# Four-layer image kernel on one Trainium2 core: group norms that hand over to the other image between their steps

## The chip, the cores and the metric

The kernel runs on one core of a Trainium2 chip. The metric is device time in microseconds of one execution, lower being better. The engines named below are PE (matrix products; PEld is its weight load), DVE (vector work out of SBUF and PSUM), ACT (ScalarE: functions and scaled copies), POOL (GpSimd) and SP (SyncE, which here only issues DMA transfers).

## The reference

Four images of 32 x 32 pixels and 384 channels pass through four layers, each of the form x = x + layer(gn(x)), where gn is a group norm over 32 groups of 12 channels and all pixels of an image:

```python
def _gn(v, G=32, eps=1e-5):
    B_, H_, W_, C_ = v.shape
    g = v.reshape(B_, H_, W_, G, C_ // G)
    m = jnp.mean(g, axis=(1, 2, 4), keepdims=True)
    s = jnp.var(g, axis=(1, 2, 4), keepdims=True)
    return ((g - m) / jnp.sqrt(s + eps)).reshape(v.shape)
...
x = x + _L0_conv_ref(_gn(x), ...)
x = x + _L1_conv_ref(_gn(x), ...)
x = x + _L2_conv_ref(_gn(x))
x = x + _L3_conv_ref(_gn(x), ...)
```

Layer 0 is deformable attention: a grouped 3 x 3 convolution of the queries gives offsets, keys and values are sampled at them, and six heads of 64 channels attend over 1024 x 1024 positions with a sampled bias. Layer 1 is attention with twelve heads of 32 channels, whose weights are multiplied by a group similarity (twelve heads are worked in six pairs). Layer 2 divides a squared box sum by a box sum of squares. Layer 3 gives each pixel a softmax over its 3 x 3 neighbourhood, applied to values and added back. All is float32, and no image depends on another.

## The kernel before

The images are independent, so the program runs two of them side by side. The *front* computes layer 0 of one image (`Front.layer0`), the *trunk* computes layers 1 to 3 of the image before it (`Trunk.image`). Layer 0 of image 0 comes first, with part of image 1's front. Then trunk 0 runs beside front 1, trunk 1 beside front 2, trunk 2 beside front 3, and trunk 3 alone.

Both sides are Python generators. A `yield n` ends a piece of the program and says that it is worth n steps. `Net.layer3` weaves the two: after each piece of the trunk it emits pieces of the front until the front is a tenth of an image ahead, counting 1109 steps for a trunk and 714 for a front:

```python
for w in self.trunk.image(b, out):
    self.done += w / TRUNK_STEPS
    while self.ahead < self.done + LEAD:
        self.ahead += next(self.fronts, 1.0)
```

The order in which instructions are emitted is not yet the order on an engine. A scheduler takes emission as priority: on each engine it places, at each point, the earliest emitted instruction that by its own reckoning is ready and has room for its output, so later pieces can fill in. On the chip each engine then runs its queue strictly in the placed order. Buffers are tiles in pools, and an allocation waits until the former holder of the space is done with.

A group norm is `Lane.norm_steps` (L342 to L394), itself a generator with a bare `yield` between steps. Where the statistics are not given it first takes them on DVE, three channel blocks (`stats`, L328 and L329). Then two small steps on DVE (L357, L358), seven tiny products on PE with the group matrix `gmat`, which sum the statistics over groups (L362), three places to hand over, the mean and variance on DVE (L372 to L375), a square root on ACT (L378), four places to hand over, the reciprocal (L380), and for each of three channel blocks a place to hand over and the normalisation on DVE (L386). `Lane.norm` runs all of it without a handover.

The norms of the program and what stands around them:

- Trunk, layer 1 (`image`): norm in place in the tile `whole`, as one piece, 15 steps. Then `inputs1`: three gate products (`dense_t`, L407) with nine filter taps each, query and key products (L1396) and so on. Then six pairs (`pair`): for each of eight key blocks j two half turns of 7 steps, with the products of queries and keys (L1699) into a two-bank PSUM tile `big`, of which there are two; exponentials (L1707); products of similarities (L1729); the weighting (L1736); products with the values (L1671). Beside it, for the next pair, `sums_step` makes products into `big` (L1561), their maximum on DVE (L1570) and the exponential's sum on ACT (L1574), which frees `big`.
- Trunk, layer 2: `out1` adds the layer 1 output (L1803, L1815) and takes the statistics; norm into `xp` as one piece, 15 steps; sums of neighbours on DVE (L1838) and PE (L1845), box products (L1870), and the result added to x (L1912, L1913) with the statistics for layer 3.
- Trunk, layer 3: norm into `xh` as one piece; products with `Wa` (L1935) and their copy (L1942); only then 15 steps; softmax, value products (L421), the sum over neighbours (L2058). At its end `start` loads the next image's x and `gmat`.
- Front, `normed`, images 2 and 3: loads of the image (L583), 24 transposes (L604) with copies (L609), a store of x on ACT's queue (L613), the norm, all as one piece of 25 steps; then transposes of the normalised image (L628) and stores (L642). Then three projections (L407), three convolution pieces (L667, 36 products and 15 steps each), and later the heads: four window pieces of 6 steps each (POOL gathers, ACT and DVE interpolate, L956 to L971, products L968), a maximum, then exponentials and value products (L1001 to L1003). Two half heads of 38 steps take as long by the weights as one pair. After every second head the sums are divided (`over_sums`). `outputs0` ends a front: output products (L407), residual loads (L491), addition (L496) and stores (L497).

The front's image 1 has its norm inside `Early`, beside image 0, and hands over there already (`alone`).

Of the kernel before, what the change touches and what calls it, by code (L numbers as in the profile page):

```python
# [27 lines left out]
NB, HW, C = 4, 32, 384  # L28
# [401 lines left out]
class Front(Lane):  # L430
# [146 lines left out]
    def normed(self, b):  # L577

        nc = self.nc
        xin = self.wt([P, NJ, C], "a12", 2)  # L580
        src = self.a["x"][b].rearrange("(j p) c -> p j c", p=P)
        for j in range(0, NJ, 2):
            nc.sync.dma_start(xin[:, j : j + 2, :], src[:, j : j + 2, :])  # L583
        if b == 0:
            early = self.early_lane
            early.gm, early.wq = self.weights("gmat"), self.weights("w_q")
            early.taps = [self.conv_weights(0)]
            self.net.more_consts()
            self.windows()
            next(self.early)  # L590
            early.taps += [early.conv_weights(1), early.conv_weights(2)]
        if b == 0:
            x = self.net.first = self.net.trunk.whole()[1]
        else:
            x = self.wt([P, KC, N], "a12", 2)

        alone = b == 1
        if alone:
            for _ in range(4):
                yield  # L600
        for j in range(NJ):
            ps = self.bank()
            for k in range(KC):
                nc.tensor.transpose(  # L604
                    ps[:, k * P : (k + 1) * P], xin[:, j, k * P : (k + 1) * P], self.ident
                )
            if alone:
                yield
            nc.scalar.copy(  # L609
                x[:, :, j * P : (j + 1) * P], ps[:, 0:C].rearrange("p (k n) -> p k n", k=KC)  # L610
            )
        if b > 0:
            nc.scalar.dma_start(self.x0[b % 2].rearrange("(k p) n -> p k n", p=P), x)  # L613
        xh = self.wt([P, KC, N], "a12", 2)
        gmat = self.gm if b == 1 else self.early_lane.gm if b == 0 else None
        for _ in self.norm_steps(x, xh, None, gmat):
            if alone:
                yield
        if b == 0:
            self.borders()  # L620
        yield 25


        pv = self.pairs[b % 2].rearrange("(g s) (y c) -> y s g c", g=G, y=2)
        for j in range(NJ):
            ps = self.bank()
            for k in range(KC):
                nc.tensor.transpose(  # L628
                    ps[:, k * P : (k + 1) * P], xh[:, k, j * P : (j + 1) * P], self.ident
                )  # L630
            if alone:
                yield
            if b == 1:
                xn = self.wt([P, C], "xn", 2)
            else:
                if j % 4 == 0:
                    four = self.wt([P, G, 2, 2 * GC], "gat", 3)
                    four = four.rearrange("p g l c -> p (g l c)")
                xn = four[:, j % 4 * C : (j % 4 + 1) * C]
            nc.scalar.copy(xn, ps[:, 0:C])  # L640
            for y, first in ((0, HW + 1), (1, 1)):
                nc.sync.dma_start(  # L642
                    pv[y, first + j * P : first + (j + 1) * P],
                    xn.rearrange("p (g c) -> p g c", g=G),
                )
        return xh
# [667 lines left out]
class Trunk(Lane):  # L1314
# [16 lines left out]

    def image(self, b, out):
        x, gmat = self.begun
        self.norm(x, x, None, gmat)
        self.xh = x
        yield 15
        with self.scope("l1y"):


            self.q4, self.k4 = self.wt([P, N], "q4"), self.wt([P, N], "k4")  # L1340
            self.xg = self.wt([P, N], "xg")
            yield from self.layer1(b)
            yield from self.layers23(b, out)
# [476 lines left out]
    def layer2(self):  # L1820
        nc, v = self.nc, self.nc.vector
        with self.scope("l2"):
            xp = self.wt([P, KC, HW, HW + 4], "xp")
            for lo in (0, HW + 2):
                nc.gpsimd.memset(xp[:, :, :, lo : lo + 2], 0.0)
            self.norm(self.x, xp[:, :, :, 2 : 2 + HW], self.mv[0])
            yield 15
            band = self.weights("band")
            num, den = [], []

# [34 lines left out]
            def box20(src, ko):  # L1865
                ps = self.big()
                near = [k for k in range(KC) if abs(k - ko) <= 1]
                for q in range(2):
                    for k in near:
                        nc.tensor.matmul(  # L1870
                            ps[:, q * 512 : (q + 1) * 512],
                            band[:, k, ko * P : (ko + 1) * P],
                            src[k][:, q * 512 : (q + 1) * 512],
                            start=k == near[0],
                            stop=k == near[-1],
                        )
                return ps
# [32 lines left out]
            for ko in range(KC):  # L1910
                psn, dn, x = box20(num, ko), dns[ko], self.x[:, ko, :]
# [6 lines left out]
    def layer3(self, b, out):  # L1918
        nc, v = self.nc, self.nc.vector
        skew = self.skew[b % 2]  # L1920
        with self.scope("l3"):
            xh = self.wt([P, KC, N], "xh")
# [2 lines left out]
            apad = self.wt([81, PW, PW], "apad")  # L1925
            nc.gpsimd.memset(apad, 0.0)
            w = self.weights("Wv")
            self.norm(self.x, xh, self.mv[1])
            attn = self.wt([P, NJ, 81], "attn")
            mt = self.wt([P, NJ, C], "mt")  # L1930
            lt = mt.rearrange("p j c -> p (j c)")[0:81, 0:N]
            for h in range(2):
# [9 lines left out]
                nc.scalar.activation(  # L1942
                    lt[:, h * 512 : (h + 1) * 512], ps, AF.Identity, bias=self.ba[:, 0:1]
                )
            yield 15
            av = attn.rearrange("p j (a q) -> p (j a) q", q=9)
            red = self.wt([P, NJ * 9], "red")
            for h in range(2):
# [204 lines left out]
```

## Time and profile before

| | us |
|---|---|
| runs shown | 4333.46, 4356.05, 4359.73 (median 4356.05) |
| profiled execution, device time | 4376.54 |
| its span | 4374.6 |
| PE busy | 3934.7 |
| DVE busy | 3109.3 |
| ACT busy | 2306.0 |
| mean granted PE clock | 0.954 |

Layer 0 of image 0 takes the first 514 us, up to the first normalisation of trunk 0 (L386 into `whole`). The next such normalisations are at 1580.0, 2655.4 and 3684.6 us, so a trunk with a front beside it takes 1066, 1075 and 1029 us and the last trunk alone some 690.

In the views below a line of the timeline reads: start, duration, engine, line, operation, output<-inputs, shape, count, and in brackets the idle time of that engine before it and what ended it. A line of the waits reads: who waited <- for whom, total us, times, longest. A float32 product shows as two instructions in the profile. Idle time matters only on the engine that holds the others up at that place.

### The profile page before, as it was taken

Reading aid. Unit: us, or ns where it says so; the run is one execution under the profiler, and the core shown is the slowest. Engines: PE = TensorE matmul, PEld = TensorE weight load, DVE = VectorE, ACT = ScalarE, POOL = GpSimd, SP = SyncE. Lnnn points to the kernel's source line nnn. Section 1 sums busy time; section 2 is a strip of 40 time slices with the busy share of each in tenths; the row PEclk is TensorE's granted clock in tenths of the full one; section 3 lists DMA queues with packets and bytes.
Section 4 is the critical chain, followed back from the end, with each engine's and each line's share of the span. In section 5 each row is a group of like instructions: output and inputs, shape, how many; then the busy total and the mean of one; then the engine's idle time right before and its main releaser. Section 6 shows DMA issues by size and latency. Waiting matters only on the chain.

```text
span 4374.6 us, 45298 instructions
## 1 busy us (share of the span) xinstructions
PE 3934.7 (90%) x14832; PEld 1683.2 (38%) x14832; DVE 3109.3 (71%) x5905; ACT 2306.0 (53%) x3638; POOL 959.2 (22%) x979
## 2 busy tenths in 40 slices
PE   8788989898999898889899989889989999999998
PEld 4333434333334443433333443333333334344444
DVE  4699676878787456687878836578887874566654
ACT  3276445656664334466766423366676641566633
POOL 1655152212121105221212101431121301000000
PEclk9999989999999998999999999899999999999998
DMA  7643253113221354321222154432221214311111
GB/s 159 220 124 119 75 177 95 55 48 93 55 85 40 123 137 146 110 64 42 78 57 80 40 158 142 130 100 61 57 79 47 74 34 135 103 38 30 33 33 43
DMA packets 295397, 385.08 MB, mean 88 GB/s; under 512 B 167858, under 2 KB 228798, under 8 KB 294650
## 3 DMA queue, kind: packets, MB, share of 16 engines
q1 hardware_dynamic: 246336, 217.44, 17.7%
q0 software_dynamic: 39936, 145.53, 11.3%
q10 hardware_dynamic: 8890, 19.23, 1.3%
q8 instruction: 118, 1.93, 0.2%
q14 instruction: 117, 0.96, 0.1%
HBM read 295.63 MB, written 86.75 MB: 87 GB/s over the span
## 4 chain that ended last, share of the span: by engine, by line
PE 50%; DVE 25%; issue 9%; ACT 9%; DMA 3%; POOL 2%; another core or an unknown queue 1%; SPq 0%; ACTq 0%; DVEq 0%; POOLq 0%
PE bank L1729 10%; PE big L1699 6%; PE big L407 5%; DVE nmax L1570 4%; PE bank L1003 4%; DVE e L1736 3%; PE big L1561 3%; ACT big L1574 3%; PE bank L421 3%; PE bank L1724 2%; PE bank L1396 2%; PE bank L1671 2%; DVE lg L962 2%; DVE z L957 2%; PE big L1870 2%
## 5 line engine op out<-in xcount | busy, mean ns | idle before, releaser
L1729 PE MATMUL bank<-whole,sg 128*128 128x512 f32 (+3 forms) x2304 | 851.7, 500 | 3.4 <-POOL sg L1682 1.8
L1736 DVE SCALAR_TENSOR_TENSOR e<-bank,gam,e 128x512 f32<-128x512 f32 x768 | 560.0, 746 | 308.7 <-PE bank L1729 184.2
L1574 ACT ACTIVATE big<-big,nmax 128x1024 f32<-128x1024 f32 x384 | 417.5, 1087 | 286.1 <-DVE nmax L1570 249.8
L1729 PEld LDWEIGHTS bank<-whole,sg 128*128 128x128 f32 x2304 | 399.6, 196 | 354.8 <-issue 272.8
L1699 PE MATMUL big<-qa,ka 64*128 64x512 f32 x1536 | 450.5, 666 | 87.8 <-ACT big L1574 84.7
L1570 DVE TENSOR_REDUCE nmax<-big 128x1 f32<-128x1024 f32 x384 | 451.8, 1216 | 68.3 <-PE big L1561 64.7
L1707 ACT ACTIVATE e<-big 128x1024 f32<-128x1024 f32 x384 | 381.8, 1020 | 176.0 <-PE big L1699 164.6
L944 POOL DMA_INDIRECT win<-strips,widx x288 | 314.3, 1091 | 697.1 <-DVE z L957 378.8
L1682 POOL TENSOR_SCALAR sg<-whole,gam 128x512 f32<-128x512 f32 x192 | 149.7, 780 | 1350.1 <-PE bank L1729 1070.4
L1561 PE MATMUL big<-k,q 32*128 32x512 f32 x1536 | 268.1, 661 | 37.5 <-issue 15.9
L1003 PE MATMUL bank<-lg,va 128*128 128x512 f32 x576 | 269.7, 610 | 13.7 <-ACT lg L1002 13.7
L751 POOL DMA_INDIRECT gat<-pairs,sidx x192 | 210.3, 1095 | 325.3 <-DVE ix_one L550 237.6
L1699 PEld LDWEIGHTS big<-qa,ka 64*128 64x128 f32 x1536 | 147.9, 197 | 344.0 <-ACT big L1574 179.1
L962 DVE SCALAR_TENSOR_TENSOR lg<-z,bias_f,lg 128x512 f32<-128x512 f32 x288 | 216.4, 768 | 49.5 <-ACT lg L961 46.8
L956 ACT ACTIVATE z<-win,bias_f 128x528 f32<-128x528 f32 x288 | 205.5, 736 | 57.4 <-DVE lg L962 26.2
L1001 DVE TENSOR_TENSOR lg<-lg,tb 128x512 f32<-128x512 f32 x288 | 181.9, 689 | 73.7 <-ACT tb L994 73.7
L957 DVE SCALAR_TENSOR_TENSOR z<-win,bias_f,z 128x528 f32<-128x528 f32 x288 | 215.0, 763 | 19.8 <-ACT z L956 11.8
L1671 PE MATMUL bank<-e,vs 128*32 128x512 f32 x1536 | 210.9, 618 | 16.8 <-DVE vs L1665 16.7
L1741 ACT COPY gn<-bank 128x128 f32<-128x128 f32 (+2 forms) x288 | 106.4, 370 | 210.6 <-DVE e L1736 209.7
L961 ACT ACTIVATE lg<-z,bias_f 128x512 f32<-128x512 f32 x288 | 199.7, 716 | 16.6 <-DVE z L957 12.1
L971 DVE TENSOR_TENSOR lg<-bank,lg 128x512 f32<-128x512 f32 x288 | 191.1, 681 | 12.1 <-PE bank L968 11.7
L968 PE MATMUL bank<-qs,kz 64*128 64x512 f32 x288 | 168.6, 669 | 13.2 <-DVE e L1736 8.3
(326 smaller groups left out, 6328.7 us busy)
## 6 DMA issues: line engine op xcount, KB each, us to landing
q<-qd SPq DMA_DIRECT2D x48, 256.0 KB
xg<-xgd SPq DMA_DIRECT2D x48, 256.0 KB
pairs<-gat SPq DMA_DIRECT2D x48, 192.0 KB
w<-in_gmat SPq DMA_DIRECT2D x15, 576.0 KB
w<-in_Wqkv SPq DMA_DIRECT2D x12, 576.0 KB
a<-in_x SPq DMA_DIRECT2D x16, 384.0 KB
q<-qpad SPq DMA_DIRECT2D x12, 512.0 KB
qs<-q SPq DMA_DIRECT2D x24, 256.0 KB
```

What stands on the lines that cost most here:

```text
L944: nc.gpsimd.indirect_dma_start(out=win, out_offset=None, in_=self.strips[:, :], in_offset=bass.IndirectOffsetOnAxis(ap=self.widx[:, q, c : ...
L957: v.scalar_tensor_tensor(z, wv[:, 1 : HH + 1, 0 : HW + 1], sc(0, 1), z, ALU.mult, ALU.add)
L962: v.scalar_tensor_tensor(lg, z[:, :, 1 : HW + 1], sc(0, 0), lg, ALU.mult, ALU.add)
L1003: nc.tensor.matmul(po, self.values_of(h, j), lf, start=j == 0, stop=j == NJ - 1)
L1561: nc.tensor.matmul(ps[r][:, h * 512 : (h + 1) * 512], self.q4[rows, i * P : (i + 1) * P], self.k4[rows, 0:512], start=True, stop=True,)
L1570: top = v.tensor_reduce(nmax[:, r, i : i + 1], ps[r], AX.X, ALU.max, negate=True)
L1574: nc.scalar.activation(ps[r], ps[r], AF.Exp, bias=nmax[:, r, i : i + 1], accum_out=den[:, r, i : i + 1],)
L1671: nc.tensor.matmul(av[r0 : r0 + HD1, :], vs[:, r, :], es[h][:, r, :], start=j == 0, stop=j == NJ - 1,)
L1699: nc.tensor.matmul(ps[:, r, :], ka[rows, j * P : (j + 1) * P], qa[rows, cols], start=True, stop=True,)
L1707: nc.scalar.activation(e, ps, AF.Exp)
L1729: last = nc.tensor.matmul(ps[:, (mid - i0) * P :], sg[:, r, m, :], sim[:, h, r, m, (mid - i0) * P :], start=m == 0, stop=m == 1,)
L1736: v.scalar_tensor_tensor(e[:, r, :], ps, self.gam[:, 1:2], e[:, r, :], ALU.add, ALU.mult, accum_out=tot[:, r, h : h + 1],)
```

## The change

The trunk's three norms, and the front's norm for images 2 and 3, now hand over at each place that `norm_steps` offers: 13 places where the norm takes its own statistics (trunk layer 1, front), 10 where they are given (layers 2 and 3). The step weights are 1 per place in layer 1 (13 in all, 15 before), 1.5 in layers 2 and 3 (15 in all), and 2 in the front (26 in all, 25 before). In layer 3 the piece with the `Wa` products keeps 2 steps. The counts 1109 and 714 by which the two sides are paced stay.

```diff
@@ -616,9 +616,12 @@
         for _ in self.norm_steps(x, xh, None, gmat):
             if alone:
                 yield
+            elif b > 1:
+                yield 2
         if b == 0:
             self.borders()
-        yield 25
+        if b < 2:
+            yield 25
@@ -1331,9 +1334,9 @@
     def image(self, b, out):
         x, gmat = self.begun
-        self.norm(x, x, None, gmat)
+        for _ in self.norm_steps(x, x, None, gmat):
+            yield 1
         self.xh = x
-        yield 15
         with self.scope("l1y"):
@@ -1823,8 +1826,8 @@
-            self.norm(self.x, xp[:, :, :, 2 : 2 + HW], self.mv[0])
-            yield 15
+            for _ in self.norm_steps(self.x, xp[:, :, :, 2 : 2 + HW], self.mv[0]):
+                yield 1.5
             band = self.weights("band")
@@ -1925,7 +1928,8 @@
             w = self.weights("Wv")
-            self.norm(self.x, xh, self.mv[1])
+            for _ in self.norm_steps(self.x, xh, self.mv[1]):
+                yield 1.5
             attn = self.wt([P, NJ, 81], "attn")
@@ -1942,7 +1946,7 @@
-            yield 15
+            yield 2
             av = attn.rearrange("p j (a q) -> p (j a) q", q=9)
```

Lines behind the first edit stand three further down in the changed kernel (L1835 becomes L1838), from layer 3's product with `Wa` on four (L1935 becomes L1939).

## The prediction

> **What bounds the kernel now.** I read the page first, then PE's waits, then the stretches around the norms, then PE's order in time there.
>
> ```profile
> span 4374.6 us, 45298 instructions
> ...
> PE 3934.7 (90%) x14832; PEld 1683.2 (38%) x14832; DVE 3109.3 (71%) x5905; ACT 2306.0 (53%) x3638; POOL 959.2 (22%) x979
> ```
>
> PE is busy for 90% of the span, so an edit that only reorders work can save no more than PE's idle time, 4374.6 - 3934.7 = 440 us, and what a lower clock costs. PE's waits, longest in total:
>
> ```profile
> PE big L1699 <- ACT big L1574: 84.7, 46, 5.1
> ...
> PE bank L1935 <- DVE xh L386: 13.9, 4, 3.5
> PE bank L362 <- DVE gn_mv L358: 13.7, 4, 5.6
> ...
> PE bank L362 <- issue: 8.8, 2, 4.4
> ...
> PE big L407 <- DVE whole L386: 4.3, 2, 2.1
> ```
>
> The norms (L362, and readers of L386) are small entries. The largest entry belongs to the six attention pairs of layer 1, where a product waits for PSUM that ScalarE frees. PE around the layer 3 norm of image 0, with the norm of image 2 (the layer 0 side, "front" below) behind it:
>
> ```profile
> 1477.26 1.70 PE L362 MATMUL bank<-gn_mv,w 128*128 128x2 f32 x14 [0.37 <-DMA w<-in_gmat]
> 1482.44 7.68 PE L1935 MATMUL bank<-xh,Wa 128*81 128x512 f32 x12 [3.49 <-DVE xh L386]
> 1489.96 2.98 PE L604 MATMUL bank<-ident,a 128*128 128x128 f32 x24
> 1497.35 3.09 PE L362 MATMUL bank<-gn_mv,w 128*128 128x2 f32 x14 [4.41 <-issue]
> ```
>
> Two holes, 3.49 and 4.41 us: each norm is one piece, and PE has nothing else in its queue. SyncE's queue in the same place:
>
> ```profile
> 1478.24 0.34 SPq L497 DMA_DIRECT2D x<-res  x1
> 1478.99 0.37 SPq L257 DMA_DIRECT2D w<-in_w_q  x1
> 1482.46 1.92 SPq L583 DMA_DIRECT2D a<-in_x  x4
> ```
>
> and what the DMA engines did then (columns: stretch, its length, busy time of PE, PEld, DVE, ACT, POOL, granted clock, DMA share, GB/s):
>
> ```profile
> 1485.60:1488.40 2.80, 2.80 (x6) 0.97 (x5) 0.00 (x0) 0.68 (x1) 0.00 (x0) 0.72 1.00 375
> 1488.40:1490.00 1.60, 1.60 (x6) 0.48 (x5) 0.00 (x0) 0.00 (x0) 0.00 (x0) 1.00 0.01 2
> ```
>
> The load of the next front image (L583) starts 4.2 us after the last store of the front before it (L497) and moves data until 1488.4. That matters below.
>
> **The change, part by part.** No instruction is added or removed: all engines keep the same number of each, activation table loads included. In the built programs PE's order differs in 208 stretches, DVE's in 364, ACT's in 232, SP's in 78, POOL's in 26. Durations below are from the profiled execution, 4376.5 us on the device; the median of the three runs is 4356.05, so a sum made on it is multiplied by 4356.05/4376.54 = 0.9953 at the end.
>
> Layer 1 norm, images 1 and 2. Before, PE has the third convolution piece (L667, 7.96 us) right behind the norm's sums and never idles. By the step weights that piece now comes due only after the first gate product (L407), and in the built order L407 stands right behind the sums. It must wait for the norm. Image 3, which has no front, shows the price: 2.12 us (the L407 entry above, two cases, 4.3 us). The clock there:
>
> ```profile
> 1580.00:1590.00 10.00, 10.00 (x72) 3.76 (x65) 2.25 (x3) 1.27 (x2) 4.97 (x6) 1.00 0.46 135
> ...
> 3676.00:3686.00 10.00, 7.88 (x34) 5.41 (x33) 6.58 (x18) 0.30 (x1) 0.00 (x0) 0.97 0.38 123
> 3686.00:3696.00 10.00, 10.00 (x21) 4.29 (x21) 0.87 (x2) 2.17 (x2) 7.25 (x8) 0.86 0.18 68
> ```
>
> Covered (image 1, first line) it is 1.00; uncovered (image 3) 0.97 and 0.86, so 0.3 + 1.4 = 1.7 us of PE work are lost. 2 x (2.1 + 1.7) = +7.6. The lower end is 0.
>
> The Trainium skill ("TensorE: Matmul & The Clock Gate", section "HAM oscillation — how this bites in real kernels") says that gaps above about 3.4 us are what halves the clock. By it a hole of 2.1 us costs no clock and this term would be +4.2. The row speaks against it.
>
> Layer 2 norms, images 0 to 2. The norm's sums now stand in the middle of eight front products (L1003) instead of behind them. Before, the readers (L1845) wait 2.25 us, three times 6.8, at clocks of 0.83, 0.83 and 0.66 over 10 us (1.7 + 1.7 + 3.4 = 6.8 us). With four products, 8 passes x 0.44 = 3.5 us, moved behind the sums that hole can close. But the sums may now wait for their statistics: from the last L1803 (ended 1384.45) to the second gn step (ended 1389.29) were 4.8 us, and only 3.5 us of products stand there, 1.3 too few. Ends: -13.6 and 3 x 1.3 = +3.9. Since the front's DVE work stays in between, I take -0.5 each, -1.5.
>
> Layer 3 norm and front norm, image 0. The new order puts the 24 transposes (L604) ahead of L1935 to fill the hole. They need the loads, which stay behind the same store: first quarter there at about 1485.6 (384 KB at 343 GB/s from 1484.3), last at 1488.4. From 1479.0 to the end of the last quarter's transposes (1488.4 + 2.98/4 = 1489.2) PE has 10.2 us with 2.98 of work: 7.2 idle, against 3.49 + 4.41 = 7.9. The front's sums come after L1935 and the value products (L421, 9.34 us) and no longer wait. -0.7. One long hole in place of two also spares one of two stretches of 6.8 us at half clock (0.72, 0.94 and 0.66 over 1476 to 1506): -3.4, at worst 0.
>
> The same, image 1. Before: 1.04 + 3.48 + 4.40 = 8.9 idle. After, the norm's sums stand behind only two L407 (4 passes, 1.8 us) after the last box product, while their statistics took 4.5 us there in image 0 (1471.74 to 1476.27): 2.7 idle. Fourteen L407 follow, then the transposes: from the last L407 (ended 2552.3) to the end of the loads (2563.5) and the last quarter (0.75) are 12.0 us, 9.0 of them idle. 11.7 - 8.9 = +2.8, and -3.4 of clock as above: -0.6.
>
> Image 2, layer 3 (no front left). Six L407 (5.3 us) now stand behind the sums and cover the 3.49; the clock there was 0.66 over 10 us: -3.5 - 3.4 = -6.9.
>
> SP: in image 0 the load of the group matrix (gmat) moves ahead of the residual loads (L491) and waits there for the last band product; the residuals took 5.1 us to arrive, and six L407 (5.3 us) cover that. 0, and 5.1 if not. Queued behind are the stores of L497 and the loads of L583.
>
> Attention pairs, images 0 to 2. Layer 1's norm now counts 13 steps, not 15, and each front image 715, not 714. In the pairs the front therefore lags by 2 trunk steps in image 0, 3.6 in image 1, 5.1 in image 2, out of 7 per half turn: some 30, 50 and 70% of the front's pieces move by one half turn. No trace shows that order. But the old pairs themselves lie at two lags, as the front's division of its sums takes 3.1 steps after the second pair: PE idle is 14.1 and 13.1 in pairs 1 and 2, 14.3 and 10.7 in pairs 3 and 4. Lag moves the mean by 1.1 us per pair; 15 pairs, 16 us either way. I take 0.
>
> Sum: 7.6 - 1.5 - 4.1 - 0.6 - 6.9 = -5.5. 4376.5 - 5.5 = 4371.0, times 0.9953: 4351. Ends: best 0 - 13.6 - 4.1 - 0.6 - 6.9 - 16 = -41, worst 7.6 + 3.9 - 0.7 + 2.8 - 3.5 + 5.1 + 16 = +31: 4315 to 4387.
>
> **Rivals.** *All holes close* (faster): if the loads arrive in time and the pieces fit, the idle time goes: 15.8 in the layer 3 pairs of norms, 3.5 in image 2, 6.8 in layer 2, together 26; and the clock behind it, 6.8 + 5.1 + 3.4 + 6.8 = 22. -48: 4308. For it: pieces do land in the holes. Against: L583 behind L497, and the lost cover in layer 1.
>
> *The pairs get worse* (slower): front work on DVE delays the maxima (L1570), ScalarE frees PSUM later (L1574), and L1699 waits. Price: the old pairs differ by 14.33 - 10.66 = 3.7 us; 15 times 55 us: 4376.5 - 5.5 + 55, times 0.9953: 4405. It decides from (43.6 + 5.5)/15 = 3.3 us per pair, or 27 waits of the present mean (84.7/46 = 1.84). For it: the largest wait is of this kind. Against: lags already present differ by only 1.1.
>
> *The scheduler filled these holes already, and nothing changes*: 4356. The order differs, and the holes are there; little speaks for it.
>
> **The numbers.** 1%, 43.6 us, is about what a measurement of this kernel can tell from no change. Forecast 0.50, no effect 0.06, all holes close 0.20, pairs worse 0.24. So within 1%: 0.56, faster 0.20, slower 0.24. The likeliest case is 4351 with 4315 to 4387; to leave out no more than 2 in 10, the range goes past both rivals: 4300 to 4410.
>
> **What would show it.** Layer 1 norms of images 1 and 2: L407 waits 2.1 us for L386. Image 0, layer 3: L604 waits some 6.6 us for L583, and neither L1939 (the old L1935) nor the front's L362 waits. Pairs: 117 to 124 us each, L1699 waiting 70 to 100 us in all. Wrong if pairs move by more than 3 us each, or if L604 finds its data at once.

## The result, and the profile after

The changed kernel takes 4398.46 us (median of 6 runs, 4390.75 to 4404.67), the kernel before, measured beside it, 4344.99 (6 runs, 4331.74 to 4359.73). The ratio is 1.0123, with an interval of 1.0104 to 1.0142: slower by 53.5 us. The time lies inside the predicted range, but only because that was drawn wide enough to take in the rivals: the likeliest case (4351, within 1%) did not happen. The rival "the pairs get worse" had 4405.

The page of the changed kernel (span, then busy time and instructions of each engine):

```profile
span 4392.7 us, 45243 instructions
...
PE 3933.9 (90%) x14832; PEld 1689.1 (38%) x14832; DVE 3111.1 (71%) x5905; ACT 2314.6 (53%) x3638; POOL 966.6 (22%) x979
```

Each engine's count is that of before and its busy time within 1%; what changed is mostly waiting. PE's waits (total us, times, longest), line numbers are three higher from L622 on and four from L1929 on:

```profile
PE big L1702 <- ACT big L1577: 88.8, 61, 4.4
PE big L1564 <- ACT big L1577: 34.0, 13, 7.0
PE bank L993 <- POOL diag L991: 28.7, 29, 5.8
PE bank L604 <- DMA a<-in_x: 25.9, 3, 11.3
PE bank L1006 <- ACT lg L1005: 25.8, 23, 2.4
...
PE bank L362 <- DVE gn_mv L358: 15.1, 5, 5.7
...
PE big L407 <- DVE whole L386: 8.7, 4, 2.2
```

The same entries before:

```profile
PE bank L990 <- POOL diag L988: 22.8, 29, 1.3
...
PE big L1561 <- issue: 15.9, 9, 4.1
...
PE bank L1003 <- ACT lg L1002: 13.7, 11, 2.4
...
PE big L1561 <- ACT big L1574: 8.9, 5, 4.1
...
PE bank L604 <- DMA a<-in_x: 6.9, 1, 6.9
```

Over the whole kernel the top entry hardly grew (84.7 before). The front's value products L1006 and its diagonal L993 wait longer, and so do the front's transposes L604. The sums' product L1564 seems to (34.0 against 8.9), but before the change another 15.9 us of its waits are put down to "issue", and the kernel with the handovers alone (first experiment below), which loses no time, has 27.5; of L604 it has 20.8. The waits of Wa's product fell from 13.9 to 3.5 us (image 3, which has no front), that of L362 for nothing but its place (8.8) is gone, and L407's doubled.

The places the prediction named, in PE's order. Image 0, layer 3 norm and front norm:

```profile
1480.40 1.62 PE L362 MATMUL bank<-gn_mv,w 128*128 128x2 f32 x14
1493.34 4.30 PE L604 MATMUL bank<-ident,a 128*128 128x128 f32 x24 [11.32 <-DMA a<-in_x]
1497.48 5.31 PE L1939 MATMUL bank<-xh,Wa 128*81 128x512 f32 x12
...
1512.56 1.62 PE L362 MATMUL bank<-gn_mv,w 128*128 128x2 f32 x14
```

The order is as forecast: one hole instead of two, neither L1939 nor the front's L362 waits. The hole is 11.32 us instead of some 6.6. SyncE's queue says why:

```profile
1480.59 0.38 SPq L257 DMA_DIRECT2D w<-in_gmat  x1
1482.04 0.38 SPq L257 DMA_DIRECT2D w<-in_w_q  x1
1483.83 0.34 SPq L497 DMA_DIRECT2D x<-res  x1
1489.07 1.91 SPq L583 DMA_DIRECT2D a<-in_x  x4
```

The store now starts 3.4 us after the norm's sums (1.0 before), and the load 5.2 us behind the store (4.2 before). Layer 1 norm of image 1:

```profile
1579.90 1.72 PE L362 MATMUL bank<-gn_mv,w 128*128 128x2 f32 x14
1583.86 7.08 PE L407 MATMUL big<-whole,w 128*128 128x512 f32 x12 [2.23 <-DVE whole L386]
1590.88 7.96 PE L670 MATMUL big<-qpad,w 64*64 64x512 f32 x72
```

The convolution piece L670 fell behind the product whose wait it used to cover, as forecast. The 10 us around that hole and around the one in image 2 (columns as in the stretches below):

```profile
1580.00:1590.00 10.00, 7.77 (x25) 4.21 (x26) 2.92 (x7) 1.56 (x3) 0.00 (x0) 0.83 0.37 118
...
2661.70:2671.70 10.00, 7.76 (x24) 4.25 (x24) 2.92 (x7) 1.56 (x3) 0.00 (x0) 0.66 0.38 118
```

And the five attention pairs behind the first in image 0 (stretch, its length, busy time of PE, PEld, DVE, ACT, POOL with instruction counts, granted clock, DMA share, GB/s), first before:

```profile
781.17:903.35 122.18, 108.04 (x438) 43.84 (x437) 100.39 (x196) 81.09 (x131) 26.23 (x26) 0.99 0.23 66
903.35:1026.69 123.34, 110.20 (x442) 44.27 (x441) 96.39 (x190) 77.18 (x124) 20.56 (x22) 0.96 0.20 55
1026.69:1148.88 122.19, 107.86 (x435) 43.41 (x435) 105.25 (x203) 85.86 (x138) 30.76 (x31) 0.97 0.28 80
1148.88:1267.76 118.88, 108.22 (x439) 43.11 (x441) 93.31 (x188) 77.55 (x124) 20.03 (x20) 0.96 0.17 49
1267.76:1367.81 100.05, 93.58 (x360) 41.00 (x357) 86.12 (x180) 61.57 (x98) 26.60 (x27) 1.00 0.27 81
```

and after:

```profile
761.51:885.52 124.01, 109.78 (x439) 43.53 (x441) 100.19 (x196) 81.78 (x131) 26.24 (x26) 0.96 0.22 65
885.52:1007.88 122.36, 106.11 (x439) 42.99 (x439) 93.67 (x188) 77.49 (x124) 20.21 (x20) 0.97 0.21 55
1007.88:1138.93 131.05, 113.52 (x436) 46.67 (x435) 106.45 (x204) 86.16 (x137) 32.14 (x33) 0.90 0.27 77
1138.93:1273.69 134.76, 119.51 (x451) 48.21 (x450) 97.59 (x195) 79.06 (x126) 18.39 (x19) 0.92 0.15 42
1273.69:1370.01 96.32, 91.57 (x347) 39.92 (x346) 83.75 (x176) 61.08 (x97) 28.26 (x27) 1.00 0.27 84
```

Two pairs grow by 8.9 and 15.9 us, at clocks of 0.90 and 0.92 instead of 0.97 and 0.96. The counts barely move: 2104 PE instructions start in the five pairs of image 0 in both kernels. In images 0, 1 and 2 these stretches take 608.5, 595.4 and 610.5 us, against 586.6, 590.1 and 591.1: +46.6 us. That is most of the loss. PE's waits that differ most in these five pairs of image 0, first in the kernel that hands over but keeps the old weights (the first experiment below, same line numbers), which loses no time:

```profile
PE big L1702 <- ACT big L1577: 19.4, 9, 4.9
```

and in the changed kernel:

```profile
PE big L1702 <- ACT big L1577: 27.7, 12, 4.3
PE bank L1727 <- DVE e L1739: 7.1, 4, 2.4
```

The last of these (a product behind DVE's weighting) does not occur in the pairs of the kernel with the old weights. Inside the pairs the wait for PSUM does grow; the total over the kernel hides it.

### The profile page after: what moved, and what is told of

Same layout as the page of the kernel before. It is cut to its first block, busy times and chain, and to the rows that moved or that the text cites. A ratio compares the mean times of both kernels' runs of the same rounds, so it can differ in the third digit from the quotient of the medians.

```text
span 4392.7 us, 45243 instructions
## 1 busy us (share of the span) xinstructions
PE 3933.9 (90%) x14832; PEld 1689.1 (38%) x14832; DVE 3111.1 (71%) x5905; ACT 2314.6 (53%) x3638; POOL 966.6 (22%) x979
## 3 DMA queue, kind: packets, MB, share of 16 engines
q0 software_dynamic: 39936, 145.53, 11.2%
## 4 chain that ended last, share of the span: by engine, by line
PE 50%; DVE 28%; ACT 9%; issue 6%; DMA 4%; POOL 3%; SPq 0%; DVEq 0%; ACTq 0%; POOLq 0%
PE bank L1732 11%; PE big L1702 6%; DVE nmax L1573 4%; PE big L407 4%; DVE e L1739 3%; PE big L1564 3%; ACT big L1577 3%; PE bank L421 3%; PE bank L1727 3%; PE bank L1006 3%; PE bank L1674 2%; DVE z L960 2%; POOL gat L754 2%; PE bank L1399 2%; DVE lg L965 2%
## 5 line engine op out<-in xcount | busy, mean ns | idle before, releaser
L1732 PE MATMUL bank<-whole,sg 128*128 128x512 f32 (+3 forms) x2304 | 864.8, 506 | 12.3 <-POOL sg L1685 10.5
L1702 PE MATMUL big<-qa,ka 64*128 64x512 f32 x1536 | 467.5, 670 | 94.3 <-ACT big L1577 88.8
L1573 DVE TENSOR_REDUCE nmax<-big 128x1 f32<-128x1024 f32 x384 | 452.1, 1218 | 58.5 <-PE big L1564 58.1
L1564 PE MATMUL big<-k,q 32*128 32x512 f32 x1536 | 267.9, 652 | 42.8 <-ACT big L1577 34.0
L1006 PE MATMUL bank<-lg,va 128*128 128x512 f32 x576 | 282.4, 623 | 26.1 <-ACT lg L1005 25.8
L1702 PEld LDWEIGHTS big<-qa,ka 64*128 64x128 f32 x1536 | 150.1, 197 | 356.3 <-ACT big L1577 190.4
L1674 PE MATMUL bank<-e,vs 128*32 128x512 f32 x1536 | 207.7, 610 | 11.1 <-DVE vs L1668 11.0
L964 ACT ACTIVATE lg<-z,bias_f 128x512 f32<-128x512 f32 x288 | 202.0, 717 | 29.6 <-DVE z L960 20.5
L1744 ACT COPY gf<-bank 128x512 f32<-128x512 f32 x192 | 111.8, 582 | 194.5 <-DVE e L1739 193.9
L974 DVE TENSOR_TENSOR lg<-bank,lg 128x512 f32<-128x512 f32 x288 | 191.9, 683 | 15.5 <-PE bank L971 15.4
```

Of the source, the lines that this page charges most:

```text
L1006: nc.tensor.matmul(po, self.values_of(h, j), lf, start=j == 0, stop=j == NJ - 1)
L1564: nc.tensor.matmul(ps[r][:, h * 512 : (h + 1) * 512], self.q4[rows, i * P : (i + 1) * P], self.k4[rows, 0:512], start=True, stop=True,)
L1573: top = v.tensor_reduce(nmax[:, r, i : i + 1], ps[r], AX.X, ALU.max, negate=True)
L1702: nc.tensor.matmul(ps[:, r, :], ka[rows, j * P : (j + 1) * P], qa[rows, cols], start=True, stop=True,)
L1732: last = nc.tensor.matmul(ps[:, (mid - i0) * P :], sg[:, r, m, :], sim[:, h, r, m, (mid - i0) * P :], start=m == 0, stop=m == 1,)
```

## The experiments

In all of them "lag" means by how many trunk steps the front is later than before. Each ratio is against runs of the kernel before on the same chip, but there were four chips: 4351.69 us for the handover and pace kernels, 4378.61 for the lags of 3.6 and 5.1, the lead of 2 and the repeat, 4344.62 for lag 1, the maxima and the late tail, 4335.23 for the lags of 7 and 14. Profiles are one execution each.

**Handover and pace apart.** The change does two things: norms are cut into pieces, and their step weights change (15 to 13 in layer 1, 15 to 17 in layer 3 up to the biases, 25 to 26 for a front norm). First the pieces with the old weights (the lines in order: front, layer 1, layers 2 and 3 with ten pieces each, behind Wa):

```diff
+            elif b > 1:
+                yield 25 / 13
...
+        for _ in self.norm_steps(x, x, None, gmat):
+            yield 15 / 13
...
+                yield 1.5
...
-            yield 15
+            yield 0
```

> The changed kernel with its handovers, but with the step weights of before: 15 steps for the layer 1 norm, 15 for layer 3 with none behind the Wa products, 25 for the front's norm. Its built order on PE differs from the kernel before in 10 stretches, all at the layer 3 norms of images 0 and 1. Theory P (the shifted pace costs the time): same as before within 0.4%, 4328 to 4362 us. Theory H (the handover itself costs it: transposes that wait for their load, 25.9 us of L604 waits in the changed kernel against 6.9 before): at least 19 us slower than before, 4364 us or more.

Then the old norms, in one piece, with the new weights, all of them and by halves (front, layer 1, behind Wa):

```diff
-        yield 25
+        yield 25 if b < 2 else 26
...
-        yield 15
+        yield 13
...
-            yield 15
+            yield 17
```

> The kernel before, norms in one piece, with the changed kernel's step weights: 13 for the layer 1 norm, 17 for the layer 3 piece, 26 for the front norms of images 2 and 3. Its PE order differs from the changed kernel in 8 stretches. Theory P: as slow as the changed kernel, 1.009 to 1.015 of before, and pairs 1 to 5 of image 0 take some 20 us longer than in the kernel before. Theory H: back to the kernel before, within 0.4%.

> The kernel before with only the trunk's weights shifted: 13 for the layer 1 norm, 17 for the layer 3 piece; the front lags by 2 trunk steps in the pairs of images 0, 1 and 2 alike. Theory P, if the lag alone sets the price: pairs 1 to 5 longer by some 22 us in each of the three images (what the changed kernel shows in image 0, which has this lag), 1.010 to 1.016 of before. If the price is not a function of the lag: image 0 some 22 us, images 1 and 2 anything between 0 and 22. Theory H: as before.

> The kernel before with only the front's 26 steps for images 2 and 3: no lag in the pairs of image 0, 1.6 steps in image 1, 3.1 in image 2. Theory P: pairs of image 0 as before, images 1 and 2 together 0 to 25 us longer, 1.000 to 1.006. Theory H: as before.

Measured: handover alone 0.9991 (0.9976 to 1.0006), 4343.44 us; all new weights alone 1.0139 (1.0114 to 1.0164), 4409.74 us; only 13 and 17, 1.0076 (1.0052 to 1.0101); only 26, 1.0088 (1.0064 to 1.0112). The handover as such costs nothing that can be measured, and the new weights cost all of the loss. The two halves missed what was expected: 13 and 17 alone cost less (1.010 to 1.016 was expected; their pairs take 608.5, 605.6 and 606.4 us), 26 alone more (1.000 to 1.006; 584.9, 604.5 and 604.6). PE's order in the kernel with the handover alone, image 0, layer 3:

```profile
1458.10 1.70 PE L362 MATMUL bank<-gn_mv,w 128*128 128x2 f32 x14 [0.28 <-DMA w<-in_gmat]
1468.41 4.17 PE L604 MATMUL bank<-ident,a 128*128 128x128 f32 x24 [8.62 <-DMA a<-in_x]
1472.41 5.31 PE L1939 MATMUL bank<-xh,Wa 128*81 128x512 f32 x12
```

Holes of 3.49 and 4.41 us before became one of 8.62 (and 0.28): the 7.9 us that the new order freed went into the wait for the load. From this norm to the next image's layer 1 norm it is 99.6 us against 98.5 before.

**Lag by itself.** The constant LEAD is moved in the kernel before, which shifts the front against the trunk in all images and changes nothing else; beside it ran the kernel before once more for its profile.

```diff
-TRUNK_STEPS, FRONT_STEPS, LEAD = 1109.0, (714.0, 714.0, 714.0), 0.1
+TRUNK_STEPS, FRONT_STEPS, LEAD = 1109.0, (714.0, 714.0, 714.0), 0.1 - 5.1 / 1109.0
```

(3.6, 1, 7 and 14 in place of 5.1, and +2 for a front that is earlier.)

> The kernel before, unchanged, for a second profile of it. Pairs 1 to 5 should again take 585 to 592 us in each of images 0 to 2; the stage up to the end of pair 0 of image 0 (781.2 us in the first profile) should be near 760 if that profile was long there by chance.

> The kernel before, all weights as before, with the front's lead smaller by 5.1 of 1109 steps (LEAD 0.1 - 5.1/1109), so that the front lags by 5.1 trunk steps in the pairs of images 0, 1 and 2 alike. Theory P with the price set by the lag: pairs 1 to 5 take 605 to 612 us in each image, as in image 2 of the changed kernel, 1.010 to 1.018 of before. If instead the price hangs on the edited weights: as before within 0.4%.

> The same with a lag of 3.6 steps in all three images. If the price is set by the lag: pairs 1 to 5 take 594 to 599 us in each image, as in image 1 of the changed kernel, 1.003 to 1.008 of before, less than at a lag of 2 or of 5.1. If the price grows evenly with the lag: between the lag of 2 (1.0076) and the lag of 5.1.

> The same the other way: the front leads by 2 steps more (LEAD 0.1 + 2/1109). If lagging is what costs: as before or faster, 0.990 to 1.002. If the kernel before stands at a favourable point and any other costs: 1.004 to 1.012, pairs 1 to 5 at 595 to 610 us.

> The kernel before with the front later by one trunk step. If the cost grows evenly with the lag, some 0.4% (ratio 1.004). If it comes in jumps as pieces of the front change their half turn, anything from 0.997 to 1.010; PE's idle time in pairs 1 to 5 then moves with it, about 10 us per image for each 20 us of time.

Measured: lag 5.1 1.0234 (1.0207 to 1.0261), lag 3.6 1.0138 (1.0109 to 1.0167), lag 1 1.0088 (1.0063 to 1.0113), a lead of 2 1.0041 (1.0025 to 1.0057). One step is already dear, so the cost doesn't grow evenly. The pairs came as expected at lags 5.1 (611.1, 610.5 and 612.0) and 3.6 (598.0, 598.6 and 597.6), but both totals are above what was expected (1.010 to 1.018 and 1.003 to 1.008): at lag 3.6 the pairs take only 17.8 us more than in the repeat of before, where the median rose by 64.5. From layer 3's norm of an image to layer 1's of the next it took 123.0 and 124.5 us there, against 98.9 and 97.6. With the lead of 2 the pairs are as before (586.3, 586.1 and 590.5), so its 0.4% does not lie in them either.

The repeat of before took 4389.62 us in its one run, with pairs of 594.3, 587.8 and 594.4, two of them above the 585 to 592 expected, and its first pair ended at 791.1 us, not near 760.

Pairs 1 to 5 by lag, from the profiles (us; "clock" is the length times one less the granted clock, idle time included, so it is not to be added to the idle time; each row is one image):

| Lag | Kernel, image | Pairs 1 to 5 | Sum | PE idle | Clock |
|---|---|---|---|---|---|
| -2 | lead 2, image 0 | 120.4 123.7 123.8 121.6 96.8 | 586.3 | 60.4 | 15.4 |
| 0 | before, image 0 | 122.2 123.3 122.2 118.9 100.1 | 586.6 | 58.8 | 15.4 |
| 1 | lag 1, image 0 | 126.1 120.1 129.5 131.7 96.0 | 603.4 | 65.2 | 23.9 |
| 2 | changed, image 0 | 124.0 122.4 131.1 134.8 96.3 | 608.5 | 68.0 | 32.4 |
| 2 | 13 and 17 only, image 0 | 124.0 122.8 129.8 135.3 96.5 | 608.5 | 67.5 | 32.4 |
| 3.6 | changed, image 1 | 123.6 124.6 121.1 130.7 95.4 | 595.4 | 58.3 | 20.5 |
| 3.6 | lag 3.6, image 0 | 124.7 124.8 120.7 131.6 96.2 | 598.0 | 56.9 | 23.9 |
| 5.1 | changed, image 2 | 125.8 134.4 126.1 125.4 98.9 | 610.5 | 70.4 | 37.5 |
| 5.1 | lag 5.1, image 0 | 128.2 134.2 125.8 123.3 99.5 | 611.1 | 69.3 | 37.5 |
| 7 | lag 7, image 0 | 122.8 130.4 123.3 122.0 99.9 | 598.5 | 58.8 | 27.3 |
| 14 | lag 14, image 0 | 121.8 128.2 123.6 118.2 106.5 | 598.3 | 59.5 | 30.7 |

Rows of one lag agree pair by pair, within 2.5 us, whichever edit made the lag and in whichever image. Profiles at no lag (the kernel before twice, the handover at the old pace, the late tail below) spread from 585.2 to 594.4 per image; no image at a lag of 1 to 14 is below 595.4. So the lag sets the price of the pairs, and the changed kernel is at 2, 3.6 and 5.1, as the prediction had worked out.

**The rival's mechanism: the maxima.** The row maxima (L1570), which ScalarE needs before it frees PSUM, are left out of the kernel before, without lag and with 5.1:

```diff
-                top = v.tensor_reduce(
-                    nmax[:, r, i : i + 1], ps[r], AX.X, ALU.max, negate=True
-                )
...
-                    bias=nmax[:, r, i : i + 1],
...
-            v.tensor_tensor(d, nmax, d, ALU.subtract)
+            v.tensor_scalar(d, d, -1.0, None, ALU.mult)
```

> The kernel before without the row maxima of the first attention passes (L1570): ScalarE takes the exponential straight from PSUM with no bias, and the sums' shift is only negated. 24 reductions per image fall away on DVE, so ScalarE no longer waits for DVE before it frees a PSUM tile. Its own time is only the base of the next run. If the maxima set the pace of the pairs, it is some 2 to 4% faster than before (ratio 0.96 to 0.98); if they do not, 0.99 to 1.00.

> The same without maxima, with the front 5.1 trunk steps later. With maxima that lag cost 2.3%. If the lag costs time because front work on DVE delays the maxima and so ScalarE's freeing of PSUM (my rival 'the pairs get worse' with its mechanism), the ratio of this run to the one without lag is within 0.5% of 1. If the cost comes from something else in the pairs (the diagonal on POOL, the group norm's factors, the order of PE's own products), at least 1.5% remains.

Measured: 4239.74 us without maxima (0.9755, 0.9714 to 0.9796), 4297.87 with lag 5.1 (0.9890, 0.9851 to 0.9930). The trace counts 96 of these reductions per image, not the 24 of the expectation. The lag costs 58.1 us, 1.4%, where with maxima it cost 2.3%: clearly above the 0.5% of the maxima theory, and from the 1.5% of the other it can't be told with four runs each. In the pairs of the three images (the kernel before again and its lag 5.1 beside these two) the lag adds:

| | Pair time | PE idle | Clock |
|---|---|---|---|
| with maxima | +57.1 | +41.2 | +30.6 |
| without | +32.6 | +26.6 | +3.4 |

So about two fifths of the price in the pairs, 24.5 us, go with the maxima: 14.6 of it PE's idle time, the rest longer busy time. These are single profiles, and leaving the maxima out also reorders the queues, so the share is rough. The wait for PSUM (L1699 behind ScalarE) fits: in these pairs the lag adds 13.2 us to it with maxima, and takes 11.2 off it without. What is left is other waits. PE's waits in the whole kernel without maxima, no lag:

```profile
PE big L1695 <- ACT big L1570: 39.6, 34, 3.7
PE bank L1725 <- POOL sg L1678: 21.9, 3, 7.6
PE bank L990 <- POOL diag L988: 20.3, 26, 1.3
```

and with lag 5.1:

```profile
PE bank L1003 <- ACT lg L1002: 31.2, 24, 2.3
PE bank L819 <- DVE xn L767: 30.5, 12, 6.5
PE bank L990 <- POOL diag L988: 27.4, 18, 4.3
PE big L1695 <- ACT big L1570: 24.9, 31, 1.9
```

The trunk's wait for PSUM (L1695) falls, and the front's own products (L1003, 11.9 without the lag, and L990) reach the head of PE's queue before ScalarE and POOL have made their inputs. L819 (11.1 without the lag) waits mostly outside the pairs. Inside them the lag adds 18.5 us to L1003, 6.1 to L990, and 15.5 to the transpose of the sums (L1601) behind DVE. L1003 and L990 grew in the changed kernel too.

**Late, or out of phase?** Two more lags, of one half turn of a pair (7 trunk steps) and of a whole one (14).

> The kernel before with the front later by 7 trunk steps, one whole half turn of an attention pair. If what costs time is the place that the front's products get within a half turn (their phase against the trunk's products), a whole half turn brings the old phase back: ratio to before within 0.4% of 1 and pairs 1 to 5 at 585 to 592 us per image. If the cost comes from being late as such, it is at least that of 5.1 steps: ratio 1.02 or more and pairs at 610 or above.

> The same by 14 trunk steps, one whole turn (two half turns). By the phase theory, within 0.4% of before even if the two halves of a turn differ; by lateness, 1.02 or more. If lag 7 is dear and this one is not, the period is the whole turn.

Measured: 1.0286 (1.0251 to 1.0322) and 1.0204 (1.0170 to 1.0238). As totals these miss the phase theory, and 14 steps cost less than 7, which mere lateness does not explain. The pairs (598.5, 598.3 and 598.0 at lag 7) lie between the two theories. In image 0 lag 7 brings PE's idle time back to 58.8 us, that of before, and four of five pairs to within 3.1 us; pair 2 stays 7.1 above. But at lag 3.6, half of a half turn off, idle time is as low (56.9), so a period of a half turn is not shown. The first two of these pairs in image 0, at lag 5.1:

```profile
782.60:910.82 128.22, 112.01 (x439) 45.10 (x437) 99.93 (x196) 81.91 (x130) 25.10 (x26) 0.92 0.23 62
910.82:1045.02 134.20, 117.84 (x451) 47.35 (x449) 97.54 (x195) 79.15 (x125) 18.39 (x19) 0.94 0.19 51
```

and at lag 7:

```profile
775.82:898.64 122.82, 109.71 (x439) 44.13 (x437) 100.36 (x196) 81.47 (x131) 25.69 (x26) 0.96 0.23 65
898.64:1029.09 130.45, 118.17 (x451) 47.75 (x449) 98.12 (x195) 79.58 (x125) 17.90 (x19) 0.95 0.19 52
```

The same 439 and 451 PE instructions take 9.2 us less at the later of the two lags: where the front's products stand within the turn counts, not only how many stand in a pair. Most of lag 7's price lies outside the pairs: from layer 3's norm of an image to layer 1's of the next, 125.5 and 125.1 us against 98.5 and 97.9.

**The gain without the price.** The changed kernel gained in one place: from the last pair of image 2 to the norm of image 3 it took 157.8 us, the handover at the old pace 170.4. Only there is the front made late, behind the pairs:

```diff
             for _ in self.norm_steps(self.x, xp[:, :, :, 2 : 2 + HW], self.mv[0]):
-                yield 1.5
+                yield 1.0 if self.b == 2 else 1.5
```

(against the handover at the old pace; `self.b` is set in `image`)

> The handover at the old pace, with the front late by 5 trunk steps in image 2 alone and only from its layer 2 norm on (10 hand-overs of 1.0 in place of 1.5). If the tail of image 2 gains from the lag itself, as the changed kernel showed there (157.8 us against 170.4 from the last pair of image 2 to the norm of image 3), without any lag in the pairs, it takes 5 to 13 us less than the handover at the old pace: ratio to before 0.995 to 0.998. If the gain needs the lag in the attention pairs ahead of it, the ratio is 0.999 to 1.000.

Measured: 4327.70 us, 0.9964 (0.9946 to 0.9982). The stretch takes 155.6 us. From layer 2's norm to layer 3's, in the handover at the old pace:

```profile
3502.70:3593.00 90.30, 76.15 (x178) 32.16 (x174) 62.19 (x81) 33.95 (x38) 11.92 (x6) 0.93 0.19 62
```

and with the late tail:

```profile
3506.55:3583.03 76.48, 70.33 (x172) 29.85 (x169) 61.42 (x80) 33.73 (x38) 13.29 (x6) 0.98 0.14 45
```

Six instructions fewer, and 13.8 us less, 8.0 of it idle time: a front product (L407) no longer waits 3.9 us for DVE, nor L362 1.6 us for the group matrix, and L1006 waits 2.0 us less. This kernel is faster than the one before by 0.4%. Against the handover at the old pace (0.9991) there are only ratios from two chips, whose intervals just overlap; the gain is seen in the stretch.

## Why the prediction was wrong

The step that failed is "Attention pairs ... I take 0", with 16 us either way. The lags it worked out (2, 3.6 and 5.1) were right. Its bound was not: it took the two lags found in the old pairs as the nearest rows, saw idle time differ by 1.1 us per pair, and took that for the spread over all lags, though single pairs in the same rows differ by 3.7. The kernel before stands at a good lag; one step of lag costs 16.8 us in the table's image. It also priced idle time alone, and the same PE instructions took about as much again by longer busy time (23.7 us against the old pace, 19.7 of it lost to a lower clock). The term measured +46.6, 3.1 us per pair; the prediction's own sign of being wrong was 3.

The stages, changed kernel against the handover at the old pace, whose profile (4339.1 us) starts like the changed one's; the profile of before on record was a slow-starting one (its first pair ends at 781.2 us against 761.8):

| Stretch | us |
|---|---|
| start to the end of the first pair of image 0 | -0.3 |
| pairs 1 to 5, images 0, 1, 2 | +21.9 +3.7 +23.9 |
| last pair to the next image's layer 1 norm, images 0, 1 | -0.7 -1.1 |
| layer 1 norm to the end of its first pair, images 1, 2 | +11.2 +12.0 |
| last pair of image 2 to the norm of image 3 | -12.6 |
| the rest of image 3 | -4.4 |
| sum | +53.6 |

Norms count from their square root (L378). Of the +49.5 in the pairs 25.8 us are more idle time of PE and 23.7 longer busy time; the clock's loss, idle time included, grew by 29.0. In the pairs of the three images PE's wait for PSUM behind ScalarE (L1702) grew by 14.3 us, L1727 behind DVE's weighting by 14.6, the front's L1006 by 7.0 and L993 by 5.5, while others fell.

- *Layer 1 norms, +7.6*: the holes came as forecast, with 1.7 and 3.4 us of clock loss (1.7 forecast). Holes of 2.23 and 2.24 us (2.12 forecast), at clocks of 0.83 and 0.66 over the 10 us around them, where the handover at the old pace has no hole and 1.00: 4.5 + 1.7 + 3.4 = 9.6. The Trainium skill ("TensorE: Matmul & The Clock Gate", section "HAM oscillation — how this bites in real kernels") warns of gaps above some 3.4 us; these rows show shorter ones with a low clock, as the row chosen in the prediction did. The same page (section "A second HAM failure mode: psum-queue depth-cycling") also tells of a kernel whose clock kept switching through frequent short idles of PE between groups of products. The prediction did not draw on it, and the pairs here agree with it: 0.90 and 0.92 in the two that grew.
- *That stretch as a whole* came to +11.2 and +12.0 (273.9 and 274.6 us, against 262.7 and 262.6). How much of this is the change is open: the profile of before took 273.5 and 267.1 us there, its repeat 265.9 and 267.2. The holes alone do not show in it: the kernel with 13 and 17 alone has the same two (2.24 and 2.23 us) and takes 264.0 and 263.6. In image 1 L1564 waits for ScalarE 16.2 us in place of 9.9. With the front's weight alone the stretch is dear in image 2 (272.0, lag 3.1) and not in image 1 (262.5, lag 1.6).
- *Layer 3 and front norms*: order right, L1939 and L362 don't wait. L604's hole in image 1 was 9.20 us (9.0 forecast), in image 0 11.32 (6.6), because the store ahead of the load moved too. From layer 2's norm to the next layer 1's the two images gave -1.1 and +0.6 against the profile of before, forecast -4.6 and -1.1. In image 1 this hides two larger changes: against the handover at the old pace, layer 2's norm to layer 3's is 14.5 us shorter (75.3), and layer 3's norm to the next layer 1's 13.4 longer (112.7).
- *Image 2 behind the pairs*: forecast -6.9 and -0.5, measured -12.6 against the old pace and -13.2 against before. The lag brought it, not the handover, which alone takes 170.4 us where before took 171.0. No further front follows image 2's, and layer 3's norm to the next layer 1's stays as it was (55.2 us, old pace 55.8).
- *The rival "the pairs get worse"* was right in sign and size: it wanted 3.3 us per pair, and 15 pairs gave 46.6/15 = 3.1 against the profile of before, 49.5/15 = 3.3 against the old pace. Its mechanism was part of it: the wait that it named grew by 14.3 us in the pairs, but at lag 5.1 without the maxima 32.6 of 57.1 us stay.

What stays open: which wait decides at each lag, why pair 2 stays long at lags 7 and 14 (and pair 5 at 14), and what the lags cost outside the pairs.

## What to carry to other kernels

When two streams are woven by step counts, every weight sets a lag: work out the new lag in every later stage and treat a lag that no trace shows as a cost of unknown size, with the clock's loss on top of the idle time. Split such an edit in two, the new hand-over points and the new weights; here the first was free and the second cost 1.4%. Spend a lag only where PE has holes and nothing behind them pays it back: here behind the pairs of image 2, the last with a front beside it.

## What the runs showed of the hardware

The clock falls in stretches without long gaps. In pair 4 of image 0 with the handover at the old pace, PE's longest wait was 2.4 us and the granted clock 0.96; in the changed kernel 2.7 us and 0.92. Where nothing covers the layer 1 norm, PE idles 2.1 to 2.6 us behind the norm's tiny products (L362); in images 1 to 3 of all profiles together 30 of 31 such holes come with 3.4 or 6.8 us at half clock at or around them (the other is in image 2 of the kernel with 13 and 17 alone). Where the convolution covers it, as in images 1 and 2 of the kernel before, the clock is 1.00.

The sum of the idle time does not fix the clock's loss. Over the pairs of three images 25.8 us more idle time went with 29.0 us more of it in the changed kernel, 26.6 with 3.4 in the pair of kernels without maxima; and two profiles of the kernel before lost 58.0 and 80.2 us at 174.6 and 168.2 us of idle time.

Profiles with the same PE order up to there ended the first pair at 761.8 us (the handover at the old pace), 781.2 and 791.1 (the kernel before, twice), so a difference of 20 us between two profiles need not come from an edit.
